# Four-layer graph network on 2708 nodes: loads of weights and of adjacency rows at other times, and other buffers for the gathered rows of the last layer

## The chip, the cores and the metric

The kernel runs on one core of a Trainium2 chip, as one launch. The metric is the device time of one execution in microseconds (us). A core has TensorE (PE, the matrix engine), VectorE (DVE), ScalarE (ACT), GpSimd (POOL) and SyncE (SP, which issues transfers). Each engine carries out its own list of instructions strictly in order, and semaphores make one engine wait for another. Sixteen DMA engines move data between device memory and the core; transfers are issued here from SP, ACT and POOL.

## The reference

The input is x (2708 x 512), the adjacency adj (2708 x 2708, sparse, non-negative, with a full diagonal) and the weights of the layers. Each layer normalises each row of x, applies ReLU, and adds its result to x:

```python
# layer 0
mask = adj > 0
head = mask / maximum(sqrt(sum(mask * mask, -1)), eps)
inc = adj + head
x = x + (inc @ h) / sum(inc, -1)
# layer 1: attention with 8 heads of 64, masked by adj: atts - 1e16 * (1 - max(adj, I))
keys, queries, values = h @ Wk, h @ Wq, h @ Wv      # per head
atts = softmax(queries @ keys.T / 8 - 1e16 * (1 - adj))
x = x + atts @ values @ Wo
# layer 2
h = relu(adj @ (h @ W1) + b1); h = relu(adj @ (h @ W3) + b3)
x = x + tanh(h @ Wf + bf)
# layer 3
hidden = h @ W + b
x = x + ((adj != 0) @ hidden) / sum(adj != 0, 0)
```

In layer 1 a softmax with a term of 1e16 times the adjacency picks one column, that of the row's largest adjacency value. The kernel therefore takes one row of values for each node (a gather by the index of the row maximum) and checks at run time that the shortcut holds; flags of these checks collect in a tile named bad, and a general path under a run-time branch stands behind the last layer.

## The kernel before

Rows are worked in 22 tiles of 128 (the last has 20 rows). The 512 features are four chunks of 128. Because adj is sparse, each output tile's sum over neighbours is split: a dense part over the first six tiles of nodes (DENSE = 6, those with most neighbours), and a listed part, in which the remaining neighbours of a tile are listed in chunks of 128 columns, their feature rows are gathered by indirect transfers from POOL into buffers (1 transfer a chunk), and the matching columns of the transposed adjacency multiply them. The program is written against a framework of tiles that has a scheduler: the source says what is computed with which buffers, and the order on each engine is chosen by the scheduler from it and can differ from the order of the source. A buffer's name is its place: two tiles of the same name and pool wait for each other.

**Layer 0** loops over tiles m = 0 to 21. For row m + some tiles ahead, row_norm (L505) takes the adjacency slab "ar" (128 x 2708, three buffers), counts its positive values with two passes of ACT (Sign L510, Relu L515), and finds the norm; row_sum takes the sum on ACT (L529); attended (L534) finds the row's maximum and its index for layer 1 on DVE (MAX8 L542, FIND_INDEX8 L544). Ranks and searches build the lists of neighbours (idx_g, idx_a), incidence builds the columns, PE sums them (L778), then norm makes hn (L186, ACT) and after(m) turns it by PE (L192), evicts it with ReLU as hT (L193, ACT), multiplies it by wvo (L158) and stores y. wvo is Wv times Wo, worked out in the first 50 us: load_values (L430) loads Wv head by head and Wo from ACT's queue; value_weights (L438) turns Wv by PE's transposes (L445), copies them on DVE (L446), multiplies and copies on ACT (L450).

Six tiles, LATE = 3, 4, 5, 0, 1, 2, are needed at once at the start, so that their second sign pass and their row maximum are put off: from m = 15 on, count_signs (Sign L497, Relu L498) and attended take them one for each m, their slabs being loaded a second time at L797 to L803. At m = 15 score_bound (L453) loads Wq and Wk and squares them on ACT (L464), for one of the checks. At m = 17 W1 is loaded into "wr" and split by split_w (L209) into three parts wa0 to wa2 for products of high precision, by ACT (L197, L207) and DVE (L199, L204); then W3 is loaded. A small DVE copy named behind (L162) writes one element of a buffer from a tile of the current m, so that what follows on that buffer cannot start earlier.

**Layers 1 and 2** take the gathered y, normalise, project with the split weights (project3, L900), and sum twice over neighbours (aggregated, L984 and L987).

**Layer 3** is prepared while layer 2's last tiles run: wb0 to wb2 hold the split W of layer 3 until the last project3, wa0 to wa2 hold the split Wf. gather_h gathers rows of hidden (hidr) by POOL (L935) for the listed chunks; room() (L1126) says where each gathered chunk goes:

```python
quad = wset.tile([P, NCD, D], FP, name="wr")
...
while True:
    for _ in range(NGG):                 # 8 buffers "gg"
        yield gathered()
    quad = wsetb.tile([P, NCD, D], FP, name=f"wb{i % 3}")
    i += 1
    for c in range(NCD):
        yield quad[:, c, :]
```

listed_products split each gathered chunk into a high and a low part (split_h, L1111 on ACT and L1113 on DVE) and multiply (L1171). Some tiles have no lists and take whole tiles instead: load_full (L1218) loads the rest of hidden from SP into wa0, wa1, wa2 and wr (line L1222), and full_steps splits them into gs1 to gs5 and multiplies; it yields so that these steps fall between the listed tiles. The listed tiles run in the order order_3; the first three have seven chunks each.

Of the kernel before, what the change touches and what calls it, by code (L numbers as in the profile page):

```python
# [42 lines left out]
def kernel(  # L43
# [165 lines left out]
    def split_w(pool, raw, tag):  # L209

        w = [pool.tile([P, NCD, D], FR, name=f"{tag}{i}") for i in range(3)]
        for c in range(NCD):
            split_b(*(part[:, c, :] for part in w), raw[:, c, :])
        return w
# [9 lines left out]
    with tc.tile_pool(name="l0_slab", bufs=2) as slabs, tc.tile_pool(  # L224
# [202 lines left out]
        wv = wset.tile([P, NCD, D], FP, name="wa0")  # L427
        wo = wset.tile([P, NCD, D], FP, name="wa1")

        def load_values():  # L430
            for h in range(H):
                nc.scalar.dma_start(
                    out=wv[:, :, h * DK : (h + 1) * DK],
                    in_=wv_d[h].rearrange("(c p) k -> p c k", p=P),
                )
            nc.scalar.dma_start(out=wo, in_=wo_d.rearrange("(c p) k -> p c k", p=P))

        def value_weights():  # L438
# [3 lines left out]
            for r in range(NCD):  # L442
                pt = ps_tr.tile([P, NCD, P], FP, name="pt")
                for c in range(NCD):
                    nc.tensor.transpose(pt[:, c, :], wv[:, c, r * P : (r + 1) * P], ident)  # L445
                nc.vector.tensor_copy(wvt[:, r, :], pt.rearrange("p c k -> p (c k)"))  # L446
# [6 lines left out]
        def score_bound(last):  # L453


            sq = hp.tile([P, 2], FP, name="sq")
            for i, src in enumerate((wq_d, wk_d)):
# [5 lines left out]
                )  # L463
                nc.scalar.activation(wqk, wqk, AF.Square, accum_out=sq[:, i : i + 1])  # L464
# [28 lines left out]
        def count_signs(m):  # L493

            sgn = slabs.tile([P, N], BF, name="sgn", bufs=GROUP)
            cnt, sum_sgn = (wp.tile([P, 1], FP, name=name, bufs=4) for name in ("cnt", "sum_sgn"))
            nc.scalar.activation(sgn, slab[m], AF.Sign, accum_out=sum_sgn)  # L497
# [161 lines left out]
        late = list(LATE)  # L659
# [17 lines left out]
        def stats_to(m):  # L677


            while normed[0] <= order_n.index(m):  # L680
# [18 lines left out]
                if t in late:  # L699
# [66 lines left out]
        for m in range(NT):  # L766
# [30 lines left out]
            if m + 8 > NT and late:  # L797
                if late[0] not in slab:
                    load_slab(late[0])
                if len(late) > 1:  # L800
                    load_slab(late[1])
                count_signs(late[0])
                attended(late.pop(0))  # L803
# [3 lines left out]
            if m == NT // 2 + 4:  # L807
                score_bound(xt[:1, :1])
# [3 lines left out]
            if m == NT // 2 + 6:  # L812
                wr = load_w(wset, w1_d, "wr", lambda w: behind(w[:1, 0, :1], xt[:1, :1]))
                w1 = split_w(wset, wr, "wa")
# [311 lines left out]
    def room():  # L1126
# [3 lines left out]
        for c in range(NCD):  # L1130
            yield quad[:, c, :]
        i = 0
        while True:
            for _ in range(NGG):
                yield gathered()
            quad = wsetb.tile([P, NCD, D], FP, name=f"wb{i % 3}")
            i += 1
            for c in range(NCD):
                yield quad[:, c, :]

# [626 lines left out]
```

## Time and profile before

| What | Value |
|---|---|
| Runs of the kernel | 1499.95 us median of 3 (1498.87 to 1506.9) |
| Profiled execution | 1489.76 us, span 1488.0 us |
| PE busy | 1298.3 us (87%), 4430 matmuls |
| DVE busy | 946.2 us (64%) |
| ACT busy | 690.3 us (46%) |
| POOL busy | 657.6 us (44%) |
| Mean granted clock of PE | 0.941 |
| Read / written in device memory | 284.58 MB / 63.29 MB |

Layer 0 takes about the first 523 us, layer 3's own products start about 1291 us and end close to the span's end, with layers 1 and 2 between. The profile is of one execution. In a timeline, a row has the start, the length, the engine, the line, the operation, the tile written and the tiles read, and in brackets the time for which the engine had been idle, with what released it; "issue" means that the wait is for nothing that the profile shows there. Rows of the view of windows have the stretch, its length, and the busy time of PE, of PE's weight loads, of DVE, ACT and POOL with the number of instructions, then PE's granted clock, the busy share of the DMA engines, and what they moved in GB/s.

### The profile page before, as it was taken

Reading aid. Unit: us, or ns where it says so; the run is one execution under the profiler, and the core shown is the slowest. Engines: PE = TensorE matmul, PEld = TensorE weight load, DVE = VectorE, ACT = ScalarE, POOL = GpSimd, SP = SyncE. Lnnn points to the kernel's source line nnn. Section 1 sums busy time; section 2 is a strip of 40 time slices with the busy share of each in tenths; the row PEclk is TensorE's granted clock in tenths of the full one; section 3 lists DMA queues with packets and bytes.
Section 4 is the critical chain, followed back from the end, with each engine's and each line's share of the span. In section 5 each row is a group of like instructions: output and inputs, shape, how many; then the busy total and the mean of one; then the engine's idle time right before and its main releaser. Section 6 shows DMA issues by size and latency. Waiting matters only on the chain.

```text
span 1488.0 us, 15510 instructions
## 1 busy us (share of the span) xinstructions
PE 1298.3 (87%) x4430; PEld 774.4 (52%) x4430; DVE 946.2 (64%) x1932; ACT 690.3 (46%) x1051; POOL 657.6 (44%) x673
## 2 busy tenths in 40 slices
PE   3987687878958849988999999899999999877997
PEld 1333233333423337745665666466666666555776
DVE  3685776869969769743343446365666656665686
ACT  5965543463256246432333334344445444554453
POOL 1254366565754432054544442244334335326652
PEclk9997789899989979999999999999999999988999
DMA  9977887978797498366777777756555666557885
GB/s 349 375 244 249 268 272 242 315 242 247 250 341 284 145 308 279 131 220 209 252 222 233 237 233 234 243 176 187 174 173 170 195 195 202 175 193 221 275 261 159
DMA packets 200056, 349.04 MB, mean 235 GB/s; under 512 B 26406, under 2 KB 113024, under 8 KB 196229
## 3 DMA queue, kind: packets, MB, share of 16 engines
q1 hardware_dynamic: 149177, 200.80, 40.7%
q0 software_dynamic: 46032, 145.05, 31.2%
q10 hardware_dynamic: 4752, 2.10, 0.6%
q8 instruction: 37, 0.61, 0.2%
q14 instruction: 58, 0.48, 0.1%
HBM read 284.58 MB, written 63.29 MB: 234 GB/s over the span
## 4 chain that ended last, share of the span: by engine, by line
PE 51%; issue 5%; DMA 3%; DVE 2%; another core or an unknown queue 2%; POOL 1%; ACT 1%; SPq 0%; DVEq 0%; ACTq 0%; POOLq 0%
PE aggs L987 14%; PE main L900 9%; PE agg L984 8%; PE mixed L900 4%; PE aggs L984 4%; PE pt L875 3%; PE agg L1171 2%; PE aggs L1171 2%; DMA raw<-in_adj_t_dram 1%; PE aggs L999 1%; PE agg L900 1%; PE pt L1171 1%; POOL wb L935 1%; PE mixed L1171 1%
## 5 line engine op out<-in xcount | busy, mean ns | idle before, releaser
L987 PE MATMUL aggs<-gg,ac 128*128 128x512 f32 (+1 forms) x520 | 232.3, 594 | 3.4 <-DMA gg<-g1d,idx_g 3.4
L935 POOL DMA_INDIRECT gg<-g2d,idx_g x130 | 131.1, 1008 | 220.2 <-PE aggs L987 170.7
L935 POOL DMA_INDIRECT gg<-g1d,idx_g x130 | 133.9, 1030 | 180.1 <-PE aggs L987 109.0
L778 PE MATMUL acc<-h,inc 128*128 128x512 f32 (+1 forms) x348 | 171.1, 632 | 19.6 <-DVE inc L630 14.1
L562 POOL DMA_INDIRECT ac<-in_adj_t_dram,idx_a x130 | 127.9, 984 | 133.4 <-DMA lst<-ac 62.3
L987 PEld LDWEIGHTS aggs<-gg,ac 128*128 128x128 f32 (+1 forms) x520 | 97.9, 189 | 110.6 <-issue 103.0
L580 POOL DMA_INDIRECT h<-h0d,idx_g x111 | 117.2, 1056 | 57.0 <-issue 28.7
L971 ACT ACTIVATE a_hi<-raw 128x384 fp32r<-128x384 f32 x84 | 43.6, 520 | 167.3 <-issue 92.2
L778 PEld LDWEIGHTS acc<-h,inc 128*128 128x128 f32 (+1 forms) x348 | 66.7, 201 | 99.0 <-issue 81.5
L984 PE MATMUL agg<-ghi,a_hi 128*128 128x512 f32 x252 | 114.8, 456 | 3.3 <-ACT a_hi L971 2.4
L158 PE MATMUL yacc<-wvo,hT 128*128 128x512 f32 (+1 forms) x176 | 91.0, 663 | 28.8 <-issue 23.3
L778 PE MATMUL acc<-h,incl 128*128 128x512 f32 (+1 forms) x222 | 102.3, 609 | 0.0
L984 PE MATMUL agg<-glo,a_lo 128*128 128x512 f32 x252 | 102.2, 405 | 0.0
L972 DVE TENSOR_TENSOR a_lo<-raw,a_hi 128x384 fp32r<-128x384 f32 x84 | 47.3, 563 | 85.3 <-ACT a_hi L971 51.0
L984 PE MATMUL aggs<-gs,a_s 128*128 128x512 f32 x252 | 100.3, 401 | 0.6 <-DVE gs L204 0.6
L935 POOL DMA_INDIRECT gg<-hidr,idx_h x65 | 68.5, 1053 | 51.1 <-issue 11.3
L881 DVE SCALAR_TENSOR_TENSOR v_lo<-pt,v_hi 128x512 fp32r<-128x512 f32 (+1 forms) x88 | 56.5, 664 | 41.8 <-ACT v_hi L880 23.4
L862 DVE SCALAR_TENSOR_TENSOR u<-aggs,u 128x512 f32<-128x512 f32 x42 | 28.9, 687 | 77.9 <-PE aggs L987 68.3
L158 PEld LDWEIGHTS yacc<-wvo,hT 128*128 128x128 f32 (+1 forms) x176 | 35.2, 209 | 77.4 <-issue 66.1
L778 PEld LDWEIGHTS acc<-h,incl 128*128 128x128 f32 (+1 forms) x222 | 42.9, 195 | 54.4 <-issue 53.0
L880 ACT ACTIVATE v_hi<-pt 128x512 fp32r<-128x512 f32 (+1 forms) x88 | 48.6, 578 | 45.6 <-PE pt L875 35.8
L542 DVE MAX8 top<-ar 128x8 f32<-128x2708 f32 (+1 forms) x22 | 65.4, 2971 | 0.0
(307 smaller groups left out, 2812.3 us busy)
## 6 DMA issues: line engine op xcount, KB each, us to landing
ar<-in_adj_dram SPq DMA_DIRECT2D x27, 1354.0 KB
raw<-in_adj_t_dram SPq DMA_DIRECT2D x122, 192.0 KB
slot<-x SPq DMA_DIRECT2D x41, 256.0 KB
at<-in_adj_t_dram SPq DMA_DIRECT2D x27, 384.0 KB
ranks<-rank_b SPq DMA_DIRECT2D x20, 485.0 KB
ac<-lst SPq DMA_DIRECT2D x16, 384.0 KB
h<-in_x_dram SPq DMA_DIRECT2D x21, 256.0 KB
h0d<-h POOLq DMA_DIRECT2D x21, 256.0 KB
```

The lines of the kernel that those rows point to most:

```text
L158: nc.tensor.matmul(acc[:n], hT[:, c, :n], w[:, c, :], start=(c == 0), stop=(c == NCD - 1))
L542: nc.vector.max(top[:n], ar[:n])
L562: nc.gpsimd.indirect_dma_start(out=ac[:, c, :n], out_offset=None, in_=adj_units, in_offset=bass.IndirectOffsetOnAxis(ap=idx_a[:, m, c0 + c ...
L580: nc.gpsimd.indirect_dma_start(out=g, out_offset=None, in_=h0d[:, :], in_offset=bass.IndirectOffsetOnAxis(ap=idx_g[:, m, c : c + 1], axis=0),)
L778: nc.tensor.matmul(acc[:n], a, g, start=(i == 0), stop=(i == len(pairs) - 1))
L880: nc.scalar.activation(hi[d], pt[d], AF.Relu, scale=UP)
L881: nc.vector.scalar_tensor_tensor(lo[d], pt[d], 0.0, hi[d].bitcast(FP), op0=ALU.max, op1=ALU.subtract)
L900: nc.tensor.matmul(acc[:n], a[:, c, :n], b[:, c, :], start=first and c == 0, stop=last and c == NCD - 1,)
L935: nc.gpsimd.indirect_dma_start(out=gs[c], out_offset=None, in_=gd[:, :], in_offset=bass.IndirectOffsetOnAxis(ap=index[:, m, c : c + 1], ax ...
L984: nc.tensor.matmul(acc[:n], a[:k, i, :n], b[:k], start=st, stop=sp)
L987: nc.tensor.matmul(mixed[:n], a, g, start=(c == 0 and not dense_of(m)), stop=(c == len(chunks) - 1),)
L1171: nc.tensor.matmul(bank_h(m)[: rows(m)], a, b, start=(i == 1), stop=(i == total))
```

## The change

Four places change. (1) Wv is loaded by one transfer, with a row order in which each partition reads 1 KB pieces, and is turned by 32 ordinary matmuls against the identity, two heads into one bank, instead of 16 transposes; the copy out of PSUM restores the order of rows. (2) The loads of Wq and Wk move to m = 11 and the squares to m = 13; W1's load moves to m = 14 and its split to m = 16, with a small behind copy ahead of each of its four chunks. (3) The late slabs are loaded one for each m from 14 to 19, and counted and searched one m later; a behind copy on the sign's output ties each to the tile of that m. (4) After wr and one round of gg, gathered rows of layer 3 go to gs1 to gs5, and from then on to wa0 to wa2 and gg in turn; the whole tiles of hidden go to wb0, wb1, wb2 and wr.

```diff
-    def split_w(pool, raw, tag):
+    def split_w(pool, raw, tag, first=None):
         w = [pool.tile([P, NCD, D], FR, name=f"{tag}{i}") for i in range(3)]
         for c in range(NCD):
+            if first:
+                first(w[0][:, c, :])
             split_b(*(part[:, c, :] for part in w), raw[:, c, :])
...
-        wv = wset.tile([P, NCD, D], FP, name="wa0")
+        wv = wset.tile([P, H, NCD, DK], FP, name="wa0")
...
         def load_values():
-            for h in range(H):
-                nc.scalar.dma_start(
-                    out=wv[:, :, h * DK : (h + 1) * DK],
-                    in_=wv_d[h].rearrange("(c p) k -> p c k", p=P),
-                )
+            nc.scalar.dma_start(
+                out=wv.rearrange("p h c k -> p h (c k)"),
+                in_=wv_d.rearrange("h (p c) k -> p h (c k)", c=NCD),
+            )
...
                 for c in range(NCD):
-                    nc.tensor.transpose(pt[:, c, :], wv[:, c, r * P : (r + 1) * P], ident)
-                nc.vector.tensor_copy(wvt[:, r, :], pt.rearrange("p c k -> p (c k)"))
+                    for k in range(0, P, DK):
+                        head = wv[:, (r * P + k) // DK, c, :]
+                        nc.tensor.matmul(
+                            pt[k : k + DK, c, :], head, ident, start=True, stop=True
+                        )
+                nc.vector.tensor_copy(wvt[:, r, :].rearrange("k (p c) -> k c p", c=NCD), pt)
...
-        def score_bound(last):
+        def load_scores(last):
...
+                scores.append(wqk)
+
+        def score_bound(last):
+            sq = hp.tile([P, 2], FP, name="sq")
+            for i, wqk in enumerate(scores):
+                behind(sq[:1, i : i + 1], last)
                 nc.scalar.activation(wqk, wqk, AF.Square, accum_out=sq[:, i : i + 1])
...
-        def count_signs(m):
+        def count_signs(m, last):
...
+            behind(sgn[:1, :1], last)
             nc.scalar.activation(sgn, slab[m], AF.Sign, accum_out=sum_sgn)
...
-            if m + 8 > NT and late:
-                if late[0] not in slab:
-                    load_slab(late[0])
-                if len(late) > 1:
-                    load_slab(late[1])
-                count_signs(late[0])
-                attended(late.pop(0))
+            step = m - (NT - 8)
+            if 0 <= step < len(LATE):
+                load_slab(LATE[step])
+            if 0 < step <= len(LATE):
+                count_signs(LATE[step - 1], xt[:1, :1])
+                attended(LATE[step - 1])
...
-            if m == NT // 2 + 4:
+            if m == NT // 2:
+                load_scores(xt[:1, :1])
+            if m == NT // 2 + 2:
                 score_bound(xt[:1, :1])
...
-            if m == NT // 2 + 6:
+            if m == NT // 2 + 3:
                 wr = load_w(wset, w1_d, "wr", lambda w: behind(w[:1, 0, :1], xt[:1, :1]))
-                w1 = split_w(wset, wr, "wa")
+            if m == NT // 2 + 5:
+                w1 = split_w(
+                    wset, wr, "wa", lambda w: behind(w[:1, :1], xt[:1, :1])
+                )
                 wr = load_w(wset, w3_d, "wr")
...
         quad = wset.tile([P, NCD, D], FP, name="wr")
         for c in range(NCD):
             yield quad[:, c, :]
+        for _ in range(NGG):
+            yield gathered()
+        for t in range(1, DENSE):
+            yield gp.tile([P, D], FP, name=f"gs{t}")
         i = 0
         while True:
-            for _ in range(NGG):
-                yield gathered()
-            quad = wsetb.tile([P, NCD, D], FP, name=f"wb{i % 3}")
+            quad = wset.tile([P, NCD, D], FP, name=f"wa{i % 3}")
             i += 1
             for c in range(NCD):
                 yield quad[:, c, :]
+            for _ in range(NGG):
+                yield gathered()
...
-            quad = wset.tile([P, NCD, D], FP, name=("wa0", "wa1", "wa2", "wr")[i])
+            pool, name = ((wsetb, "wb0"), (wsetb, "wb1"), (wsetb, "wb2"), (wset, "wr"))[i]
+            quad = pool.tile([P, NCD, D], FP, name=name)
```

More of the change, by code (lines that the diff above doesn't have):

```diff
@@ L451, in value_weights @@
             return wvo
-        def score_bound(last):
-            sq = hp.tile([P, 2], FP, name="sq")
+        scores = []
+        def load_scores(last):
             for i, src in enumerate((wq_d, wk_d)):
@@ L658 @@
         order_n = ZERO[:1] + FIRST + ZERO[1:] + list(range(LEAD + GROUP, NT))
-        late = list(LATE)
         normed, near, far = [0], [LEAD], [LEAD]
@@ L698, in stats_to @@
                     masks.clear()
-                if t in late:
+                if t in LATE:
                     slab.pop(t)
```

## The prediction

> **What bounds the kernel now.** I read the page's totals first, then the slices, then each engine's timeline where the slices show TensorE (PE) below 9.
>
> ```profile
> span 1488.0 us, 15510 instructions
> PE 1298.3 (87%) x4430; PEld 774.4 (52%) x4430; DVE 946.2 (64%) x1932; ACT 690.3 (46%) x1051; POOL 657.6 (44%) x673
> PE 51%; issue 5%; DMA 3%; DVE 2%; another core or an unknown queue 2%; POOL 1%; ACT 1%; SPq 0%; DVEq 0%; ACTq 0%; POOLq 0%
> ```
>
> PE is busy 1298.3 of 1488.0 us, so all that scheduling can recover is the 190 us in which it is not, plus a little slow clock. The change leaves layers 1 and 2 (about 521 to 1278 us) in the same order on every engine, so I looked for PE's holes elsewhere: the start, the last tiles of layer 0, and the start of layer 3. The view of windows (length; busy time of PE, PEld, DVE, ACT, POOL; granted clock, DMA share, GB/s):
>
> ```profile
> 0.00:25.00 25.00, 7.43 (x27) 4.17 (x28) 6.83 (x19) 8.71 (x10) 4.53 (x21) 1.00 1.00 331
> ...
> 420.00:440.00 20.00, 6.99 (x16) 3.11 (x15) 12.55 (x17) 14.11 (x12) 11.37 (x12) 0.66 1.01 395
> ...
> 460.00:480.00 20.00, 15.22 (x34) 6.89 (x33) 18.12 (x40) 10.55 (x13) 6.63 (x7) 0.83 0.95 363
> ...
> 1300.00:1320.00 20.00, 11.35 (x43) 7.76 (x42) 11.88 (x26) 11.40 (x17) 0.00 (x0) 0.84 0.58 196
> ```
>
> Between 420 and 440 PE has 7 us of work in 20, with the DMA engines saturated; between 1300 and 1320 POOL does nothing at all. The timelines (start, length, instruction, idle before and releaser) name the causes. At the start ACT has no work for 5.3 us:
>
> ```profile
> 15.69 2.44 ACT L529 ACTIVATE ar<-ar 128x2708 f32<-128x2708 f32 x1
> 18.04 0.19 ACT L529 ACTIVATION_READ_ACCUMULATOR ar<-ar 128x1 f32 x1
> 23.52 0.20 ACT L516 ACTIVATE rn<-sum_sgn 128x1 f32<-128x1 f32 x1 [5.29 <-DVE sum_sgn L513]
> ```
>
> It waits for a DVE result that stands in DVE's order behind three copies of transposed value weights (L446), the last of which waits for PE until 22.7. Late in layer 0, ACT and then PE:
>
> ```profile
> 420.11 2.46 ACT L497 ACTIVATE sgn<-ar 128x2708 bf16<-128x2708 f32 x1 [5.86 <-issue]
> ...
> 428.33 1.91 ACT L464 ACTIVATE wa<-wa 128x2048 f32<-128x2048 f32 x1 [0.64 <-issue]
> ...
> 435.45 0.60 ACT L193 ACTIVATE hT<-pt 128x512 f32<-128x512 f32 x1 [5.11 <-remote]
> ```
> ```profile
> 436.10 4.64 PE L158 MATMUL yacc<-wvo,hT 128*128 128x512 f32 x6 [13.01 <-issue]
> ...
> 472.82 1.11 PE L192 MATMUL pt<-ident,hn 128*128 128x128 f32 x4 [4.78 <-ACT hn L186]
> ```
>
> PE's transposes ended at 423.1, but their eviction hT was queued behind two late signs and one square that waited for 4.7 MB issued at 410 to 412 (two slabs, Wqs, Wks): a 13.0 us hole. The 4.78 us one has the same form: hn behind a sign that waited 5.5 us for its slab. At the start of layer 3, POOL and PE:
>
> ```profile
> 1289.27 1.34 POOL L935 DMA_INDIRECT gg<-hidr,idx_h  x1 [0.30 <-issue]
> 1325.22 0.95 POOL L935 DMA_INDIRECT wb<-hidr,idx_h  x1 [34.62 <-issue]
> ```
> ```profile
> 1315.90 0.79 PE L1171 MATMUL agg<-ghi,a_hi 128*128 128x512 f32 x1 [6.73 <-ACT ghi L1111]
> ...
> 1343.76 0.80 PE L1171 MATMUL aggs<-gg,ac 128*128 128x512 f32 x1 [5.12 <-DVE gg L1113]
> ...
> 1355.09 0.79 PE L1171 MATMUL agg<-wb,ac 128*128 128x512 f32 x1 [3.99 <-DVE wb L1113]
> ```
>
> The 13th gather's place is wb0, which holds weights until the last projection (1323.0 to 1324.5). So gathers at 1.255 us each start 34.6 us late, and PE runs into them.
>
> [...] after the 6.73 us hole matmuls follow each other at 0.43 us, elsewhere at 0.23. A closed hole thus returns more than its length. [...]
>
> **Part 1, value weights.** Eight loads on ACT's queue become one, 4096 packets of 256 B become 1024 of 1 KB. [...] The ACT queue's packets take some 8 us of the 16 engines here; less 2.9 us for the output weight at the 362 GB/s of this stretch, Wv has 5.4[...]. ACT issues 7 DMAs fewer. 16 transposes (0.27 us each) become 32 matmuls of 64 rows by 128; that form isn't in the trace. The nearest are the 128x128 matmul of L619 (0.38 for two, 0.19 each) and the transpose (0.27), so 6 to 8.6 us for 4.3: up to 4.3 more, in a stretch where PE has 7.4 and then 18.1 of 25. The copies keep their size but write with a stride; between 0 and 0.5 us each more, 4 of them. The gain: in the changed order sum_sgn stands behind one such copy. ACT, which is fully busy from 23.5 to about 101 us, gets up to 5.3 us earlier. Against it, DMA is saturated to 75 us, and PE's first transpose, now behind the whole megabyte, moves from 9.0 to perhaps 13. Bounds +4 and -6; I take -4.
>
> **Part 2, other weights.** The loads of Wqs and Wks and two squares (1.91 us each) move from tile 15 to tiles 11 and 13, some 330 to 390 us. There ACT is busy 16 of 50 us and DMA is at 0.78, which hides them; uncovered they cost 4 + 2 MB at 395 GB/s = 9 us. w1's load goes from tile 17 to 14, its split (four chunks, eight DVE operations, 5.2 us by rows L199 and L204) from right behind its load to tile 16, with four tiny DVE copies (0.1 us each) added. Before, DVE waited 1.5 us for it at 479.7.
>
> **Part 3, late slabs.** Six loads (1354 KB, 3.5 us at 395 GB/s) go from two at first to one a tile, each a tile before its sign. ACT's order now has one sign, then hT and hn, per tile. The copies that delay the signs cost 0.1 us of DVE each. What goes: of 13.0 us the part that waits for data, about 5.9 + 2 + part of 5.1 on ACT; the 4.78; on DVE 1.5 and 4.8 (idle at 438.5 for ACT's sign). Sum some 18 us of PE holes, plus slow clock (0.66 in one window). But DVE is busy about 97 us between 400 and 515, and its searches and lists (MAX8, FIND_INDEX8 2.97 us each) set the pace; it has 18 us to give in all, of which the 20-row tail keeps some. So parts 2 and 3 give between 0 and -18; I take -10. Next late is DVE itself.
>
> **Part 4, places of layer 3.** Gathers 13 to 17 find gs1 to gs5 free since the last dense sum, so they issue from 1290.6 to 1297; gathers 18 on take wa0 to wa2, free when the last projection with wa ends at 1309.2. Twelve gathers at 1.255 us then end near 1324, where before the first of them began. PE's holes behind gathers (0.64, 1.57, 5.12, 3.99: 11.3 us) should nearly close, and some 25 matmuls at 0.43 instead of 0.23 give up to 5 more. The loads and casts of the full tiles (rows gs<-wa, ACT 0.62 us each) leave the place ahead of the last tile's tanh: one cast with its DMA wait and a table load stand before it, 1.5 us of the 6.73; the rest is that tile's way to HBM and back. The full loads move to wb0 to wb2, after 1325, 12 of 256 KB = 3.1 MB, 8 us at 395 GB/s, with DMA at 0.6: hidden if the full products come after the listed ones, as PE's order has them. Casts: 12 times 0.62 on ACT, 0.69 on DVE, which are half busy there. Sum -1.5 - 9 - 3 = -13.5; bounds 0 and -18. I take -13.
>
> **Sum.** -4 - 10 - 13 = -27. The profiled execution (1489.76, 1.76 around its span) would be 1463. The runs shown have a median of 1499.95, 0.7% above it; from that, 1473. [...] the "remote" waits can land elsewhere: about 6 us either way. I say 1474.
>
> **Rivals.** (a) Layer 0 gives little: DVE, and DMA at 0.95 to 1.0, take the late part's gain and the start's: -2 - 13 = -15, 1485. For: DVE's 20.00 of 20 between 480 and 500. Against: its 12.55 in the worst window. (b) Layer 3 gives little: the moved casts or wb loads keep PE waiting instead: -14 - 1, 1485. For: three holes there already end on ACT or DVE. Against: both half idle. (c) Slower: a slab load, the first thing of its tile on SP, waits for a slab buffer (three, freed by DVE's search), and all adjacency and list loads of the next tile are queued behind it. Six tiles at d us: it decides from d = 27/6 = 4.5 us, and at 6 us a tile the time is 1509. Against: the same buffers and order held two slabs before. (d) The change doesn't do what it says: not so for order, which shows the signs spread and the gathers' places moved; only that nothing waits there any more is open, 1499.
>
> **Numbers.** All parts, 1464 to 1482: 0.58. (a) 0.16, (b) 0.14, (d) 0.07, (c) 0.05. About 0.5% (7.5 us) is what a measurement here tells from no change. From the main case, (a) and (b) nearly all is faster: 0.87; same 0.08; slower 0.05. 8 in 10 lies in 1460 to 1492: the lower end has every bound (-6 - 18 - 18) mostly realised, the upper end has one part missing and 6 us of shifted waits against it.
>
> **What would show it.** Right: no PE hole above 5 us between 420 and 480; one sign a tile; no POOL wait above 12 us between 1278 and 1330; ACT's rn near 18 to 20; layers 1 and 2 of equal length. Wrong: DVE at 20 of 20 from 400 to 515 with the stage as long; PE holes at 1310 to 1360 now ending on gs casts or wb loads; new waits of some 10 us marked "remote" on PE's path.

## The result and the profile after

| What | Before | After |
|---|---|---|
| Runs, side by side | 1501.75 us median of 19 (1496.59 to 1512.4) | 1493.12 us median of 19 (1473.29 to 1505.87) |
| Ratio after/before | | 0.9926, interval 0.9901 to 0.9952: about 11 us less |
| Same pair measured again (run changed_again) | 1499.06 us median | 1486.85 us; 0.9928 [0.99, 0.9956] |
| Profiled execution | 1489.76 us | 1493.7 us |

The change gained about 11 us where 27 were forecast. Medians and ranges here and below are of all executions; the ratios, and the differences in us given with them, leave out executions that fell into a slower state. The two profiled executions can't be subtracted from each other: that of before happened to be 12 us below its median, that of after about at its median. Two profiled executions of the changed program (the second is changed_again) have spans of 1491.9 and 1481.7 us, and 9.0 of these 10.2 us lie ahead of layer 1's start. So the stages below are read for their waits, and only differences that several programs show count as lengths.

The page of the changed kernel, the lines that answer to those shown of before:

```profile
span 1491.9 us, 15610 instructions
PE 1301.6 (87%) x4478; PEld 774.6 (52%) x4478; DVE 948.3 (64%) x1944; ACT 689.1 (46%) x1051; POOL 662.4 (44%) x673
```

PE has about the same work (1298.3 us before) and is idle as long as before, 190 us. The view of windows, with the columns as before:

```profile
400.00:420.00 20.00, 17.21 (x50) 7.97 (x48) 19.73 (x45) 5.05 (x8) 16.34 (x13) 1.00 0.82 255
420.00:440.00 20.00, 17.84 (x47) 8.27 (x48) 19.88 (x41) 7.20 (x9) 15.72 (x15) 1.00 0.92 314
440.00:460.00 20.00, 17.61 (x43) 7.83 (x42) 20.00 (x31) 11.54 (x17) 16.65 (x12) 0.91 0.93 327
460.00:480.00 20.00, 20.00 (x52) 9.01 (x51) 20.00 (x45) 8.74 (x11) 7.42 (x8) 1.00 0.82 307
...
1300.00:1320.00 20.00, 13.76 (x44) 9.72 (x42) 8.43 (x18) 7.18 (x11) 3.47 (x4) 0.74 0.36 104
```

The worst window of before is repaired in this execution: from 420 to 440 PE has 17.84 us of work instead of 6.99, and no PE hole between 420 and 480 is longer than 3.45 us, where there were 13.0 and 4.8. But the third busy column, DVE, now stands at 19.7 to 20.0 of 20 in four windows in a row, and layer 0 ends no sooner: the last copy of y out of PSUM starts at 522.6 us in both (table below). At the start, ACT and then PE (timelines):

```profile
0.75 0.46 ACTq L434 DMA_DIRECT2D wa<-in_L_gnn_Wvs_dram  x1
...
7.54 2.46 ACT L524 ACTIVATE sgn<-ar 128x2708 bf16<-128x2708 f32 x1 [4.39 <-DMA ar<-in_adj_dram]
...
11.61 2.44 ACT L543 ACTIVATE ar<-ar 128x2708 f32<-128x2708 f32 x1
...
19.39 0.20 ACT L530 ACTIVATE rn<-sum_sgn 128x1 f32<-128x1 f32 x1 [5.25 <-DVE rstd L181]
23.85 0.99 ACT L284 CAST counts<-list 64x384 bf16<-64x384 f32 x2 [4.25 <-PE list L275]
```
```profile
16.27 1.98 PE L449 MATMUL pt<-ident,wa 128*64 128x128 f32 x16 [16.27 <-DMA wa<-in_L_gnn_Wvs_dram]
```

ACT starts its first row sum at 11.61 instead of 15.69, since it issues one load in 0.46 us instead of eight in 8.62. Of these 8 us only 4 arrive, because ACT now waits 4.39 us for its adjacency slab (the line at 7.54). Then it waits twice, 5.25 and 4.25 us, where before it waited once for 5.29. PE begins at 16.27 instead of 9.04, behind the whole megabyte. By the second row sum the lead is gone: 30.26 us, before 30.40. Layer 3, POOL and then PE:

```profile
1289.17 0.95 POOL L953 DMA_INDIRECT gs<-hidr,idx_h  x1 [6.56 <-PE agg L1002]
...
1324.29 1.13 POOL L953 DMA_INDIRECT wa<-hidr,idx_h  x1 [19.90 <-PE main L918]
```
```profile
1331.10 0.79 PE L1193 MATMUL agg<-ghi,a_hi 128*128 128x512 f32 x1 [5.21 <-ACT ghi L1129]
```

POOL's wait of 34.62 us is one of 19.90. Of the twelve gathers from 1289.17 to 1304.4, seven go into gg, which the kernel before also had out by 1290.6; the five into gs are gained. The next group goes to wa at 1324.29. The last projection with wb, before and after:

```profile
1325.47 1.07 PE L900 MATMUL mixed<-wb,v_s 128*128 128x512 f32 x4
```
```profile
1339.05 1.15 PE L918 MATMUL mixed<-wb,v_s 128*128 128x512 f32 x4
```

Layer 2 ends some 14 us later in this execution, so the gathers into wa begin 15.9 us ahead of the end of that projection (1340.2), where those into wb began 1.3 us ahead of it (1326.5). From there to the end of the span it takes 151.7 us, before 161.4. PE's first hole fell from 6.73 to 5.21, and the later ones of 5.12 and 3.99 behind gathers are gone.

And the end of layer 0. The last late slab on ACT, the last search on DVE, POOL's last list store (tiles 1 and 2), and PE's first instruction of layer 1, all of the changed kernel:

```profile
504.88 2.44 ACT L511 ACTIVATE sgn<-ar 128x2708 bf16<-128x2708 f32 x1
...
507.79 0.81 ACT L186 ACTIVATE hn<-xt,shift,rstd 128x512 f32<-128x512 f32 x1
508.50 2.45 ACT L512 ACTIVATE sgn<-sgn 128x2708 bf16<-128x2708 bf16 x1
...
510.95 0.58 ACT L193 ACTIVATE hT<-pt 128x512 f32<-128x512 f32 x1
```
```profile
510.87 2.97 DVE L558 FIND_INDEX8 at_top<-top,ar 128x8 uint32<-128x2708 f32 x1
...
514.02 0.20 DVE L183 TENSOR_SCALAR shift<-mv,rstd 20x1 f32<-20x1 f32 x1
```
```profile
523.46 0.59 POOL L585 DMA_DIRECT2D lst<-ac  x1 [3.65 <-DMA ac<-in_adj_t_dram,idx_a]
```
```profile
543.33 1.12 PE L893 MATMUL pt<-ident,slot 128*128 128x128 f32 x4 [20.82 <-ACT slot L186]
```

The last three of these places in the kernel before:

```profile
508.42 2.97 DVE L544 FIND_INDEX8 at_top<-top,ar 128x8 uint32<-128x2708 f32 x1
```
```profile
518.23 0.57 POOL L571 DMA_DIRECT2D lst<-ac  x1 [0.91 <-DMA ac<-in_adj_t_dram,idx_a]
```
```profile
539.11 1.11 PE L875 MATMUL pt<-ident,slot 128*128 128x128 f32 x4 [16.52 <-issue]
```

What is to be seen: in ACT's order the last late slab's two passes stand around tile 20's hn and ahead of its hT. DVE's last row-maximum search ends at 513.8 instead of 511.4 with the last tile's shift behind it, but this costs nothing here: the shift stands at 514.02 (before 514.14), and PE's products of the last tile start at 518.24 (before 518.32). Tile 20's product, before and after, starts 2.2 us sooner and takes 2.1 us longer:

```profile
513.80 3.70 PE L158 MATMUL yacc<-wvo,hT 128*128 128x512 f32 x8 [0.75 <-issue]
```
```profile
511.58 5.84 PE L158 MATMUL yacc<-wvo,hT 128*128 128x512 f32 x8 [2.19 <-ACT hT L193]
```

PE's granted clock from 500 to 515 us is 0.80 here and was 1.00. A slow product also comes in a run without the late part (5.34 us in few_before, below); the wait of about 2 us does not. Ahead of the products of tiles 18 and 20, PE waits 1.8 to 2.4 us in eight of the nine profiles that have the late slabs at the change's tiles (in late_lists_out, which arranges this end anew, it doesn't), and 0.75 us at most in the nine without part 3. There hT stands behind the second pass of a late sign, as in the lines above.

The last list is stored by POOL at 523.46 instead of 518.23, and PE's hole between the layers is 20.82 us instead of 16.52. SP shows a way from the one to the other. Its order has loads of x, which wait for the list, ahead of the last store of y (after, then before):

```profile
525.82 1.29 SPq L1056 DMA_DIRECT2D slot<-x  x3
527.16 0.36 SPq L737 DMA_DIRECT2D y<-yo  x1
```
```profile
523.27 0.30 SPq L724 DMA_DIRECT2D y<-yo  x1
```

The last y is stored 4.0 us after its copy out of PSUM has ended (523.16); before, it went at once. The copies of y out of PSUM on ACT (L722 before), one for each tile, tell when the lead is lost (start in us, from the timelines):

| Tile | 14 | 15 | 16 | 17 | 18 | 19 | 20 | 21 |
|---|---|---|---|---|---|---|---|---|
| before | 413.7 | 441.9 | 463.4 | 481.1 | 493.6 | 508.6 | 517.5 | 522.7 |
| after | 427.1 | 443.7 | 460.0 | 472.8 | 490.2 | 507.3 | 517.5 | 522.6 |
| late_again (below) | 414.2 | 439.4 | 457.9 | 470.6 | 487.1 | 504.3 | 514.8 | 520.0 |
| few_before (below) | 418.5 | 445.0 | 465.8 | 483.9 | 495.6 | 511.5 | 522.0 | 527.1 |
| few_late (below) | 421.4 | 446.1 | 461.8 | 474.5 | 489.4 | 507.3 | 517.3 | 522.5 |

From tile 14 to tile 17 the changed order wins 11 to 22 us on its counterpart (rows 2 and 3 against 1, row 5 against 4); from tile 17 to the last it gives 5 to 8 of them back.

### The profile page after: what moved, and what is told of

The parts are those of the page before. It is cut to its first block, busy times and chain, and to the rows that moved or that the text cites. A ratio compares the mean times of both kernels' runs of the same rounds, so it can differ in the third digit from the quotient of the medians.

```text
span 1491.9 us, 15610 instructions
## 1 busy us (share of the span) xinstructions
PE 1301.6 (87%) x4478; PEld 774.6 (52%) x4478; DVE 948.3 (64%) x1944; ACT 689.1 (46%) x1051; POOL 662.4 (44%) x673
## 4 chain that ended last, share of the span: by engine, by line
PE 68%; DMA 9%; DVE 7%; issue 7%; ACT 3%; another core or an unknown queue 2%; POOL 2%; SPq 1%; ACTq 0%; DVEq 0%; POOLq 0%
PE aggs L1005 14%; PE main L918 10%; PE acc L791 9%; PE agg L1002 7%; PE mixed L918 5%; PE aggs L1002 4%; PE yacc L158 3%; PE aggs L1193 3%; PE agg L1193 3%; PE pt L893 3%; PE aggs L1017 1%; PE pt L1193 1%; DMA lst<-ac 1%; PE agg L918 1%
## 5 line engine op out<-in xcount | busy, mean ns | idle before, releaser
L576 POOL DMA_INDIRECT ac<-in_adj_t_dram,idx_a x130 | 134.9, 1037 | 132.2 <-DMA lst<-ac 63.1
L791 PE MATMUL acc<-h,inc 128*128 128x512 f32 (+1 forms) x348 | 164.6, 615 | 18.1 <-DVE inc L644 10.3
L953 POOL DMA_INDIRECT gg<-hidr,idx_h x62 | 63.0, 1016 | 49.8 <-PE aggs L1193 17.2
```

Of the source, the lines that this page charges most:

```text
L576: nc.gpsimd.indirect_dma_start(out=ac[:, c, :n], out_offset=None, in_=adj_units, in_offset=bass.IndirectOffsetOnAxis(ap=idx_a[:, m, c0 + c ...
L791: nc.tensor.matmul(acc[:n], a, g, start=(i == 0), stop=(i == len(pairs) - 1))
L953: nc.gpsimd.indirect_dma_start(out=gs[c], out_offset=None, in_=gd[:, :], in_offset=bass.IndirectOffsetOnAxis(ap=index[:, m, c : c + 1], ax ...
```

## The experiments

In all, 18 runs, each timed beside the kernel before; three of them (changed_again, late_again, values_again) repeat a program. The first four ran on a chip where the kernel before takes 1417.36 us (median of 69 runs), the others on chips where it takes 1498 to 1502 us, so that only ratios are compared. The expectations speak of theory A, that what parts 2 and 3 gain is given back at the end of layer 0, where POOL gathers and stores the lists of tiles 1 and 2, and of theory B, that each part gives what was forecast.

### Each part alone, and the lists sooner

places is part 4 alone, late is parts 2 and 3, values is part 1, with the diffs shown above. lists_sooner is the whole change with one edit:

```diff
-            if m == NT - LEAD - 1:
-                for t in range(1, LEAD):
-                    gather_adj(t)
+            if m in (NT - LEAD - 2, NT - LEAD - 1):
+                gather_adj(m - (NT - LEAD - 3))
```

> Kernel before with part 4 alone (places of layer 3's gathered rows and whole tiles). Forecast of the prediction: -13 us (-0.9%), bounds 0 and -18. If the missing gain went missing in layer 0 (theory A), this run shows -10 to -14 us, with no POOL wait above 12 us between 1278 and 1330. If the moved casts and loads eat it (theory B, rival b), it shows 0 to -4 us.

> Kernel before with parts 2 and 3 alone (other weights and late slabs). Forecast: -10 us. Theory A (PE gets through the late tiles sooner, but the end of layer 0 is set by POOL's gathers of the lists of tiles 1 and 2, which didn't move, and whose last store and last gather changed places): within 4 us of the kernel before, with the last output copies of layer 0 some 5 to 15 us earlier and the first gathers into slot not earlier. Theory B: -8 to -12 us.

> Kernel before with part 1 alone (value weights in one load, turned by matmuls). Forecast: -4 us. Theory A: 0 to +4 us, since the first product of layer 0 waits for later things than the row count (the profile after has the first copies of wvo at the same times as before). Theory B: -3 to -5 us.

> Changed kernel with one edit: the adjacency lists of tile 1 are gathered by POOL one tile sooner (m = 17 instead of 18; tile 2 stays at 18). Theory A: 4 to 8 us faster than the changed kernel, since POOL's list gathers set the end of layer 0; first gathers into slot that much sooner. Theory B: no difference from the changed kernel (within 3 us).

| Run | Median (range, runs) | Ratio to before |
|---|---|---|
| places | 1407.78 (1399.31 to 1419.37, 22) | 0.9934 [0.9913, 0.9955] |
| late | 1417.83 (1413.39 to 1425.6, 22) | 1.0006 [0.999, 1.0022] |
| values | 1422.91 (1413.6 to 1431.49, 17) | 1.0046 [1.0024, 1.0068] |
| lists_sooner | 1410.93 (1404.44 to 1421.71, 21) | 0.9963 [0.9944, 0.9981] |

Of the three parts only the places gain, 0.66% or 9.4 us. The late part gives nothing that is measured, and the values cost 6.5 us. POOL's wait in the run of places is 18.02 us, and from the end of the last projection with wb to the end of the span it takes 142.9 us, against 152.0 in the run of the late part. The edit of lists_sooner turned out to exchange the places of one list store and one gather on POOL, too little to test theory A.

### The whole change, and without part 1, on another chip

without_values is parts 2, 3 and 4. The edit of the lists was put on it, and on the kernel before as a control.

> The changed kernel as it is, beside the other three on one chip. If the parts add up as measured alone (places -9, late 0, values +6): -2 to -4 us against the kernel before. If parts help each other (late and places with values): -9 to -12 us, as at first.

> The changed kernel with part 1 undone (value weights loaded head by head, turned by transposes). If part 1 costs what it cost alone: 5 to 7 us faster than the changed kernel, so -8 to -10 us against the kernel before. If part 1's cost came only from the order of the kernel before around it: no difference from the changed kernel.

> Parts 2, 3 and 4, and the lists of tile 1 gathered one tile sooner. If POOL's list gathers hold the end of layer 0 (theory A): 4 to 6 us faster than the kernel without part 1, so -13 to -16 us against the kernel before, and faster than both kernels. If not: the same as without part 1.

> Control: the kernel before with only the lists of tile 1 one tile sooner. Theory A says that there the last copies of y, not the lists, set the end of layer 0 (the last list store at 464.6, the last output copy at 472.4 us in the run with places alone), so within 3 us of the kernel before. If gathering sooner were good by itself, it shows -4 to -6 us here too.

| Run | Median (range, runs) | Ratio to before |
|---|---|---|
| changed_again | 1486.85 (1474.22 to 1500.17, 22) | 0.9928 [0.99, 0.9956] |
| without_values | 1485.0 (1469.26 to 1499.43, 19) | 0.9908 [0.9875, 0.9941] |
| without_values_lists_sooner | 1486.01 (1474.92 to 1503.08, 20) | 0.9938 [0.9908, 0.9969] |
| before_lists_sooner | 1501.39 (1485.23 to 1514.43, 22) | 1.0017 [0.999, 1.0043] |

Leaving part 1 out is as good as the whole change or better (by 4.3 us, ratio of the two 0.9971, interval by resampling their runs 0.9945 to 0.9996). Taking the lists one step sooner in the source does nothing that is measured. By their ratios the three parts alone add to about -2 us on the first chip, where lists_sooner, the whole change but for that small edit, gave -5; here the whole change gives -11. No run explains this difference. The changed kernel's second profile says something on its first: the same program, whose last list is stored at 511.81 this time, has no longer hole between the layers than the kernel before:

```profile
534.33 1.12 PE L893 MATMUL pt<-ident,slot 128*128 128x128 f32 x4 [15.49 <-issue]
```

So the 4 to 5 us of list in that gap come in some executions only: 20.8 us in the first profile of the changed kernel, in without_values 20.9 and in late on the first chip 19.2, but 15.5 here. The delay of the last y store goes with it: 4.0 us in the first two and 2.0 in late, but 0.02 in changed_again and 0.55 at most in the nine profiles without the late part.

### The late part again, with the lists moved out of the end; part 1 again, in one load and in two

late_lists_out is parts 2 and 3 with the ranks, the searches and the list gathers of tiles 1 and 2 moved ahead:

```diff
-            if m + 8 == NT + 1:
+            if m + 8 == NT:
                 todo.append(partial(rank_rows, list(range(1, LEAD))))
...
-                do_next(2 if NT - 8 < m < NT - 5 else 1)
+                do_next(2 if NT - 9 < m < NT - 5 else 1)
...
-            if m == NT - LEAD - 1:
+            if m == NT - LEAD - 2:
                 for t in range(1, LEAD):
```

values_in_two_loads splits part 1's load, so that PE's first products need 256 KB only:

```diff
-            nc.scalar.dma_start(
-                out=wv.rearrange("p h c k -> p h (c k)"),
-                in_=wv_d.rearrange("h (p c) k -> p h (c k)", c=NCD),
-            )
+            for h0, h1 in ((0, 2), (2, H)):
+                nc.scalar.dma_start(
+                    out=wv[:, h0:h1].rearrange("p h c k -> p h (c k)"),
+                    in_=wv_d[h0:h1].rearrange("h (p c) k -> p h (c k)", c=NCD),
+                )
```

> Parts 2 and 3 alone once more, as the companion of the next run on one chip. Theory A: within 5 us of the kernel before; in its profile PE's last output copies of layer 0 come sooner, and the first loads of layer 1 wait for POOL's last list store.

> Parts 2 and 3, with the ranks, searches and list gathers of tiles 1 and 2 one tile sooner, so that on POOL both lists and their stores stand ahead of the last tile's gather. Theory A: 4 to 8 us faster than parts 2 and 3 as they are, since the first loads of layer 1 no longer stand behind a list store. If DVE sets the end of layer 0 (rival a), no difference, since its work is the same.

> Part 1 alone once more, as the companion of the next run on one chip: +3 to +7 us against the kernel before, as first measured.

> Part 1 with its load in two (heads 0 and 1, then heads 2 to 7); the order of the instructions on every engine is otherwise that of part 1 alone. If part 1 loses because PE's first transposes, DVE's copies and the count behind them wait for the whole megabyte (15.9 us instead of 9.0): the first transposes start 4 to 7 us sooner and the kernel is 3 to 6 us faster than with part 1 alone. If the loss lies in the order that the scheduler makes of the later tiles: no difference.

| Run | Median (range, runs) | Ratio to before |
|---|---|---|
| late_again | 1493.6 (1485.92 to 1503.0, 14) | 0.9994 [0.9961, 1.0028] |
| late_lists_out | 1510.74 (1502.86 to 1519.8, 6) | 1.0114 [1.0045, 1.0182] |
| values_again | 1510.73 (1487.71 to 1527.04, 22) | 1.0011 [0.9973, 1.005] |
| values_in_two_loads | 1506.18 (1495.85 to 1531.19, 22) | 1.0062 [1.0036, 1.0087] |

The late part gives nothing that is measured on this chip either. With the lists ahead it is slower, by six executions: POOL's fixed list work then stands before the last tile's own adjacency gather, which starts at 497.9, and PE gets holes of 12.05 and 6.46 us at 507 and 522. The remedy of theory A fails; whether its diagnosis holds, it doesn't tell. Waiting for less of Wv changes nothing for the better either.

### Fewer list gathers, four loads, and part 1 in eight loads

The few_ kernels leave out 15 of the 19 adjacency gathers for the lists of tiles 1 and 2 (the expectations speak of 18 of 20): the first chunk of each group is gathered and stored in all the places of its group. The expectations' gaps of 20 to 24 us are measured from a point that in some traces lies before the last copy; PE's hole between the layers, which is the right measure, is 15.7 us in late_again.

```diff
-                for c in range(k):
+                for c in range(k if m not in (1, 2) else 1):
                     nc.gpsimd.indirect_dma_start(
...
-                    nc.gpsimd.dma_start(out=listed[m][:, c0 : c0 + k], in_=ac[:, :k, :n])
+                    got = ac[:, :k, :n]
+                    if m > 0:
+                        got = ac[:, :1, :n].to_broadcast([P, k, n])
+                    nc.gpsimd.dma_start(out=listed[m][:, c0 : c0 + k], in_=got)
```

four_loads is the kernel before with Wv in four loads; every instruction of PE and DVE keeps its place:

```diff
-            for h in range(H):
+            for c in range(NCD):
                 nc.scalar.dma_start(
-                    out=wv[:, :, h * DK : (h + 1) * DK],
-                    in_=wv_d[h].rearrange("(c p) k -> p c k", p=P),
+                    out=wv[:, c].rearrange("p (h k) -> p h k", k=DK),
+                    in_=wv_d[:, c * P : (c + 1) * P].rearrange("h p k -> p h k"),
                 )
```

value_matmuls is part 1 with one load for each head, in the new row order.

> The kernel before, leaving out 18 of the 20 adjacency gathers of the lists of tiles 1 and 2 (each list gets its first chunk in all its places); POOL loses some 22 us of issuing between 485 and 515 us, all else keeps its order. Control for the next run. POOL theory: in the kernel before, PE's own last copies come as late as the list, so little changes, -3 us or ratio 0.998, and the gap from the last copy to layer 1's first transpose stays near 16 us. Rival (something else holds the end of layer 0, DVE or PE's own chain): the same.

> Parts 2 and 3 alone, with the same 18 gathers left out. POOL theory: the gap from the last copy to layer 1's first transpose falls from 20-24 us to about 16, and the gain of the late tiles comes through: 5 to 8 us below the run few_before, ratio to the kernel before about 0.993. Rival (the gain is given back elsewhere, whatever POOL does): the gap stays at 20 or more, or layer 1 starts no sooner, and the ratio is that of few_before within 0.2%.

> The kernel before with Wv in four loads instead of eight (still pieces of 256 bytes), every instruction of PE, DVE and POOL in the order of before; only ACT issues four transfers fewer. If the time that ACT takes to issue is worth anything here: ACT's first row sum 2 us sooner, and -2 us. If, as the profile of the value part shows for the second row sum, the stage waits for data anyway: 1.000 within 0.2%. Neither theory gives a loss; a loss would mean that the loading itself costs.

> Part 1 with eight loads (one for each head, pieces of 1 KB) and the new matmuls and copies; the scheduler then orders later tiles as in part 1 alone (about 210 instructions of PE and DVE at other places). If the loss of part 1 comes with the matmuls, the copies or that order: as part 1 alone, 1.002 to 1.007. If it came from the one large load: 1.000 or below.

| Run | Median (range, runs) | Ratio to before |
|---|---|---|
| few_before | 1499.63 (1488.5 to 1509.79, 22) | 0.9995 [0.9967, 1.0023] |
| few_late | 1495.44 (1484.37 to 1514.41, 22) | 0.9951 [0.9924, 0.9978] |
| four_loads | 1496.77 (1487.3 to 1507.35, 22) | 0.9998 [0.9971, 1.0026] |
| value_matmuls | 1506.27 (1489.08 to 1522.73, 14) | 1.0002 [0.9967, 1.0037] |

Without these gathers the late part does gain: few_late is 6.1 us below few_before (ratio of the two 0.9959, by resampling 0.9936 to 0.9983), while leaving them out gives the kernel before nothing that is measured. Against the late part with all its gathers the step is less clear: the interval of late_again, 0.9961 to 1.0028, overlaps that of few_late, 0.9924 to 0.9978; that of late on the first chip, 0.999 to 1.0022, does not. So POOL's list work at the end of layer 0, or the transfers that it starts, takes a part of the late part's gain; how large a part is open. PE's first instruction of layer 1, in few_before and then in few_late:

```profile
542.52 1.12 PE L878 MATMUL pt<-ident,slot 128*128 128x128 f32 x4 [15.45 <-issue]
```
```profile
537.91 1.12 PE L892 MATMUL pt<-ident,slot 128*128 128x128 f32 x4 [15.51 <-issue]
```

The holes are equal, and the difference is the last copy's, 522.47 against 527.15. These two profiles would not show that the lists hold the end, and late_again with all its gathers has a hole of 15.7 us as well; only the times speak for it.

four_loads shows that fewer loads alone give nothing, and not even an earlier ACT: four loads of 256-byte pieces kept it for 9.05 us, eight for 8.62, eight of 1 KB pieces (value_matmuls) for 6.98. value_matmuls, neither better nor clearly worse than before, leaves open what part 1's loss comes from.

### The late slabs one tile sooner

In the changed order the last late slab is tied to tile 20, the last full one. These two kernels move the whole sequence one tile ahead, in parts 2 and 3 alone and with the places:

```diff
-            step = m - (NT - 8)
+            step = m - (NT - 9)
```

> Parts 2 and 3 alone, with the late slabs loaded at m = 13 to 18 and counted at m = 14 to 19 instead of 14 to 19 and 15 to 20. Theory D (the last late slab's sign passes and search hold the last two tiles): the normalisation of tile 20 and of the last tile no longer stands behind them, the last copy of layer 0 comes 3 to 6 us sooner, and the ratio to the kernel before is 0.995 to 0.998. Rival (the lists on POOL hold the end): the last copy may come sooner, but the first transpose of layer 1 does not, ratio 1.000 within 0.2%. Slower, 1.003 or more: one tile sooner the signs and searches collide with the lists' own searches on DVE.

> Parts 2, 3 and 4, without part 1, the late slabs one tile sooner as in the run late_one_sooner. Theory D: 3 to 6 us under the run without the value part, ratio to the kernel before 0.987 to 0.989. Rival: that run's 0.991.

| Run | Median (range, runs) | Ratio to before |
|---|---|---|
| late_one_sooner | 1508.58 (1501.89 to 1517.68, 17) | 1.0079 [1.0051, 1.0108] |
| places_late_one_sooner | 1498.34 (1483.55 to 1507.15, 22) | 0.9989 [0.9962, 1.0015] |

Theory D fell: both are slower than with the slabs where the change has them, by about 0.8%. The third outcome that was named is the one measured. In windows of late_one_sooner, DVE is full (the third busy column, 59.3 of 60 us):

```profile
440.00:460.00 20.00, 14.35 (x39) 6.53 (x38) 19.28 (x36) 9.39 (x13) 16.35 (x13) 1.00 0.79 253
460.00:480.00 20.00, 17.44 (x35) 7.52 (x36) 20.00 (x43) 8.52 (x11) 7.33 (x8) 0.83 0.95 364
480.00:500.00 20.00, 17.32 (x45) 7.66 (x44) 20.00 (x37) 8.50 (x12) 10.97 (x12) 1.00 0.40 129
```

Its last search starts at 508.8, as before, and the searches for the lists (2.17 us each) now share these 60 us with more of the row maxima, so that the last gather of the lists is at 522.59 and the last copy at 533.56. The pair also measures the places once more, on one chip: 10.2 us by the medians, ratio 0.9919 (by resampling 0.9899 to 0.9937).

## Why the prediction was wrong

**What bounds the kernel.** Nothing in the runs speaks against PE's idle time being what there is to win, and layers 1 and 2 stay as they were: between 540 and 1270 us no instruction of PE, DVE, ACT or SP and no transfer of POOL has another place in its order. The two layers take 747.2 us before and 754.3 after, in the other profiles on such chips 747.1 to 755.0.

**Part 4, forecast -13: right.** Alone it gave -9.4 us, beside the late part -12.3 by the means of the last pair. The mechanism is as told: gs takes the 13th to 17th gather at once, PE's hole ahead of the listed products shrinks by the 1.5 us worked out (6.73 to 5.21), and the holes of 5.12 and 3.99 behind gathers close (the one of 0.64 ended on DVE's a_hi, not on a gather). One sign failed: POOL waits 19.9 us and not under 12. The last projections, whose ends the working took as 1309.2 for wa and 1324.5 for wb (this one ended at 1326.5), end at 1325.9 and 1340.2 in the changed kernel's execution, so the gathers into wa that were to end near 1324 begin there. Measured from the last projection with wb, they have nearly the lead that was worked out, 15.9 us where 1309.2 is 17.3 ahead of 1326.5.

**Parts 2 and 3, forecast -10, measured 0 (1.0006 and 0.9994): this step failed.** The term that failed is "So parts 2 and 3 give between 0 and -18; I take -10": it counts PE's holes as time at the end of layer 0. The prediction wrote that the searches and lists on DVE "set the pace" and that "Next late is DVE itself", and then still took 10 of the 18 us that DVE had idle (16.5 by the windows, which have 98.5 us of DVE's work from 400 to 515 and not 97). What the runs show in its place is a time unchanged: 11 to 22 us are won between tiles 14 and 17, 5 to 8 of them are given back by the last tile, and the last copy of y starts 0.1 us sooner than before in the changed kernel (which stood 13 us behind at tile 14) and 2.7 in late_again.

In the changed kernel's first profile the holes closed as the working said, the 13.0 us one and the 4.78 us one both, and ACT has one late sign a tile. The first of these holes, ahead of tile 15's product, doesn't always close: it is 8.3 to 14.4 us long in the nine profiles without the late part, gone in five with it, and 3.9 to 8.5 us in five more. Where it stays, PE's transposes are done and ACT is idle, in late_again for 11.24 us with a release marked "remote", that is by another core or a queue that the profile doesn't know. The working counted a part of such a wait, "part of 5.1 on ACT", among what would go. And the new order has holes of its own, the 1.8 to 2.4 us ahead of the products of tiles 18 and 20. Further:

- DVE's idle time did not become end time. Up to 515 us it has the same work in both profiles, split at 400 us 289.98 + 98.53 us before and 280.07 + 109.87 after: in this execution it came to 400 us some 10 us behind, and the closed holes only made that good. In late_again, with 291.72 + 96.74, it is idle for 18.3 of the last 115 us, where before it was for 16.5: the idle time moved, 4.9 us of it behind 500 us where 1.9 were. Its last search starts at 508.4 before, and at 507.8, 510.9 and 508.8 in late_again, few_late and late_one_sooner (502.8 in without_values).
- The small copies were costed at "0.1 us of DVE each". Their price is the order they force. Each ties one slab to one tile, so that the last slab can't start before tile 20, and ACT's 4.9 us for it stand ahead of that tile's hT. In the kernel before, the last of these signs ran at 481.6 us, ahead of the norm of tile 18; after, at 508.5. DVE's 6 us for the last search stood ahead of the last two tiles before as well. Moving all of them one tile sooner doesn't help, since it puts the row maxima on DVE beside the list searches.
- Behind that stands POOL. The forecast named no cost for the lists of tiles 1 and 2, which the change leaves where they are; without most of these gathers the late part is worth 6 us. In some executions the last store of y also waits 2 to 4 us on SP for such a list.

That the lists take something is shown by the times of a run, not how much, and not whether it is POOL's time or the transfers. The first two are read from the traces and agree with both runs that rearranged this stage and lost by it, but no run lightened DVE or took the ties away, so they stand as argued, and how the missing 10 us divide among all these stays open. Nor is zero exact beside the other parts: without_values gave 0.92%, 13.8 us, on a chip on which the places alone, 9.4 us on the first one, were not run.

**Part 1, forecast -4: wrong in sign.** Alone it measured +6.5 us on one chip (1.0046); on another, in two loads 1.0062, and as it is 1.0011, which can't be told from no change. Within the whole change it cost 4.3 us. What was worked out came true in its parts: ACT's issues shrank, the 32 small products, 64 matmuls in the trace, took 6.7 us of PE where the transposes took 4.1, inside the 6 to 8.6 worked out, and DVE's copies went from 0.69 to 1.07 us, inside the bound. That larger pieces would take less of the DMA engines' time was the author's estimate, which the trace of before alone did not show. The runs show it: of the first 80 us the packets of ACT's queue take 10.4% of the 16 engines' time before and 7.5% after, that is 8.3 and 6.0 us, 2.3 less. It goes with the pieces and not with the number of loads: of the whole span this queue has 0.6% before and with four loads of 256-byte pieces, and 0.4% after and with eight loads of 1 KB pieces.

But PE's first transpose, which was to move "from 9.0 to perhaps 13", moved to 16.27, since one load has no first part that could land sooner (in two loads ACT's rn, which waits behind it, starts at 13.73 us and not at 19.39), and 4 us of gain on ACT met a second wait of 4.25 us for PE. That makes the gain zero at 30 us, not a loss. What makes the loss stays open: the scheduler, given other matmuls, also places over 100 other instructions of PE and some 180 of DVE elsewhere, up to about 610 us. One load, two loads and eight loads don't separate this from the matmuls themselves. In the single profiles on the first chip layer 0 is not even longer: layer 1 starts at 484.3 us in values, at 488.9 in late and at 489.6 in places.

**The rivals.** Rival (a), that layer 0 gives little because DVE takes it, at 16%, comes nearest in its number: it gave -15 and 1485 us; measured were -11 and 1493.12, and the difference is about what part 1 cost. Its cause is not shown. The sign listed under wrong, "DVE at 20 of 20 from 400 to 515 with the stage as long", is what the windows of the first profile show from 400 to 480, and the profile of before had 20.00 of 20 between 480 and 500, to which more weight belonged. But late_again gains as little with DVE at 15.4 to 18.9 of 20 in the five windows from 400 to 500, so a full DVE is not all of it. Rivals (b), (c) and (d) did not occur: no slab load held SP's queue for 4.5 us a tile, and the full tiles from wb did not keep PE waiting.

**The signs.** Of those listed for right, no PE hole above 5 us between 420 and 480, one sign a tile, and rn near 18 to 20 (19.39) came in the first profile. They are signs of repaired holes, and say nothing of when the stage ends.

**The range.** Its upper end, 1492, misses by 1.1 us. It had "one part missing"; in fact one part gave nothing that was measured and another was negative.

## What to carry to other kernels

A closed hole on the bound engine is not yet time at the end of the stage: follow the engines that feed that end (here DVE, ACT's last signs, POOL's gathers, which in late_lists_out stood behind the list work until 497.9 us, and SP's stores, the last of which went out 4.0 us late behind loads) to the stage's last instruction before turning holes into time. A copy that holds an instruction back may cost what it puts last, not what it takes to run. And when a change has parts, measure them alone: here one part made most of the gain, one gave nothing that was measured, and one took some of it back on the chip where it was clearly measured.

## What the runs showed of the hardware

- One program takes 1417 us on one chip and 1498 to 1502 us on others. Parts 2 and 3 start layer 1 at 488.92 us on the first and 535.57 on a slower one, so 47 of the 67 us between these two profiles lie in layer 0, where all 130 adjacency gathers are (PE's mean granted clock is 0.958 and 0.944 in these two). On the slower chips waits marked "remote" of 4 to 21 us stand on one or more engines between 100 and 350 us in each of the 16 profiles; in the four on the first chip none is above 3 us. Their cause was not found.
- ACT's time for issuing eight loads of 128 KB is 8.62 us, four of 256 KB 9.05 us, eight in 1 KB pieces 6.98 us, two of 1 KB pieces 0.98 us and one 0.46 us, with the same megabyte in each. That is 0.46 to 2.26 us for one load, so not one price for each issue.
- A program whose order is fixed has, from one execution to the next, a last list store at 511.8 or 523.5 us, and a gap between two layers of 15.5 or 20.8 us. Two single profiles can't show a difference of 5 us in this layer.
- A store on SP was held by loads ahead of it in SP's order that waited for something else: the last y store went out 4.0 us after its data was there, behind loads of x that waited for a list, in one execution of the changed program, and 0.02 us after in another.
